# Second layer of a two-layer graph attention: dividing by the row sums per 16 groups instead of per group, and projecting from transposed rows

## The chip, the cores and the metric

The kernel runs on one core of one Trainium2 chip, in float32 throughout. The metric is the time of one execution on the device in microseconds (us).

## The reference, cut to what matters

Two layers of attention over a graph of 4096 nodes with 512 features, 8 heads of 64 each. Only the second is touched here:

```python
h = relu(layernorm(x))                        # x: output of layer 0
keys, queries, values = per head h @ Wk, h @ Wq, h @ Wv
atts = queries @ keys.T / 8 - 1e16 * (1 - max(adj, eye))   # (8, 4096, 4096)
atts = softmax(atts, axis=-1)
x = x + einsum('hqm,hmk,hko->qo', atts, values, Wo)
```

The softmax is exp(score - extreme of the row) divided by the sum of the row. The division can be done at any time before the projection with Wo, since it is one factor per row and head.

## The kernel before, in words

The first layer, the layer norm and the projections to queries, keys and values end at about 2600 us; queries and keys lie transposed in DRAM (`qk_d`), values in `v_d`, the first layer's output in `x1_d`.

The second layer's attention works on `HC` = 4 pairs of heads c (2 x 64 = 128 rows of the transposed output), and in each on `NG` = 32 groups g of 128 query rows. A group has `GS` = 4 steps of 32 queries; so there are `total` = 512 steps. In a step the 128 partitions hold 32 queries times four quarters of the 4096 keys, and the free axis holds 1024 keys for each of the two heads. Stages of several groups overlap: in the loop over s, step s makes the scores of step s (`scores`, TensorE, L856; `masked`, VectorE, adds the penalty from PSUM into the ring `t`, L872), the exponentials of step s-3 (`exps`, ScalarE, L907, whose accumulator output is the sum of each partition), the transposes of step s-4 (`squares` on VectorE by 32x32 blocks, L914; `turned` on TensorE, L920, with the copy `taken` on ScalarE, L926), and a quarter of the product with the values for the group of step s-8 (`weighted`, L937, into one PSUM tile `o`). In every odd step the partial minima of two steps are combined over the four quarters (`parted` on POOL, L881, then `smallest`, L891 and L896). In head pair 0 the penalty is made from adj (`with_self` L838, `made_penalty` L842 and L843) and kept in DRAM (`pen_d`); the later pairs load it.

`finish` closes a group in the two steps after its last product: ScalarE copies `o` (128 rows of two heads by 128 queries) to SBUF as `oT` (L947), four small products on TensorE with `band` add the sums of the four quarters (`den`, L950), VectorE inverts them (L954), TensorE transposes `oT` (`back`, L957), VectorE multiplies (L959), and a DMA stores 128 rows by 128 columns in `att_d` (L963).

The order of instructions on every engine is the order written in the loop (`manual_schedule`); an engine that waits holds all that is written behind it. All loads and stores go through SP's queue, in order too; penalties are requested `AHEAD` = 5 steps before use, into 6 buffers `a`.

When all groups are done, a second stage projects: for each of 32 row blocks it loads `at` (L1050) and `xt` (L1048), transposes four squares of `at` on TensorE (L1053), copies them on ScalarE (L1055), multiplies by `wot` (L1058), adds on VectorE (L1061) and stores (L1062). `wot` is loaded at its start through ScalarE's queue (L1045).

Of the kernel before, what the change touches and what calls it, by code (L numbers as in the profile page):

```python
# [8 lines left out]
F32 = mybir.dt.float32  # L9
# [3 lines left out]
PSUM = bass.MemoryType.PSUM  # L13
DRAM = bass.MemoryType.DRAM

P = 128
# [7 lines left out]
def kernel(  # L24
# [14 lines left out]
    nc = tc.nc  # L39
    N, DM = x.shape  # L40
    H, D = src_proj.shape[1:]
    HD = H * D
    NB = N // P
    KC = DM // P
    HC = HD // P
# [6 lines left out]
    dram = ctx.enter_context(tc.tile_pool(name="dram", bufs=1, space=DRAM))  # L52

    ident = const.tile([P, P], F32, name="ident")
# [5 lines left out]
    SQ = 32  # L60
    NS = P // SQ
    band = const.tile([P, SQ], F32, name="band")
    nc.vector.tensor_reduce(band, ident.rearrange("p (a j) -> p j a", j=SQ), AX.X, ALU.add)
    bands = const.tile([P, P], F32, name="bands")
# [9 lines left out]
    x1_d = dram.tile([N, DM], F32, name="x1_d")  # L74
# [16 lines left out]
    PR = 2 * D  # L91
# [5 lines left out]
    with tc.tile_pool(name="a0k", bufs=1) as pk, tc.tile_pool(name="a0v", bufs=4) as pv, tc.tile_pool(  # L97
        name="a0a", bufs=3
    ) as pa, tc.tile_pool(name="a0t", bufs=7) as pt, tc.tile_pool(name="a0p", bufs=4) as pp, tc.tile_pool(
        name="a0x", bufs=1  # L100
    ) as px, tc.tile_pool(name="a0s", bufs=4) as psb, tc.tile_pool(
        name="a0tr", bufs=3, space=PSUM
# [103 lines left out]
        def finish(G):  # L206

            rows, cols = bass.ts(G.g, P), bass.ts(G.c, PR)
            xt = px.tile([P, PR], F32, name="xt")
            nc.sync.dma_start(xt, x[rows, cols])  # L210
            oT = px.tile([P, P], F32, name="oT")
            nc.vector.tensor_copy(oT, G.o[:, :P])
            den = psb.tile([P, 2], F32, name="den")
            nc.vector.reciprocal(den, G.sm)
            yield
            back = G.o[:, P:]
            nc.tensor.transpose(back, oT, ident)
            yield
            att = px.tile([P, 2, D], F32, name="att")
            nc.vector.tensor_mul(  # L220
                att, back.rearrange("p (h d) -> p h d", d=D), den.unsqueeze(2).to_broadcast([P, 2, D])
            )
            nc.gpsimd.tensor_add(xt, xt, att.rearrange("p h d -> p (h d)"))
            nc.sync.dma_start(x1_d[rows, cols], xt)
# [162 lines left out]
        groups = [Group(c, g) for c in range(PAIRS) for g in range(NB)]  # L387
        total = len(groups) * 2
# [4 lines left out]
        with tc.manual_schedule():  # L393
            NQ = NB // XR
            TB = 8
            rows = [load_rows(0)]
            wn, col = load_wn()
            rows.append(load_rows(1))
            for q in range(NQ + 4):
# [10 lines left out]
                n = q - 3  # L410
# [14 lines left out]
            for s in range(total + 6):  # L425
                G, h = step(s) if s < total else (None, 0)
                for half in range(2):
# [8 lines left out]
                    q = 2 * s + half  # L436
# [320 lines left out]
            while jobs:  # L757
                work()
    l0.close()
    att_d = dram.tile([N, HD], F32, name="att_d")  # L760
    pen_d = dram.tile([N // 32, P, N // 4], F32, name="pen_d")

# [5 lines left out]
    VC = 768  # L770
    NV = VC // SQ
    NT = (QK_ - VC) // P
    with tc.tile_pool(name="a1t", bufs=1) as pt, tc.tile_pool(name="a1k", bufs=4) as pkk, tc.tile_pool(
        name="a1v", bufs=GS
    ) as pv, tc.tile_pool(name="a1a", bufs=6) as pa, tc.tile_pool(name="a1q", bufs=2) as pq, tc.tile_pool(
        name="a1x", bufs=1
    ) as px, tc.tile_pool(name="a1s", bufs=6) as psb, tc.tile_pool(
        name="a1sc", bufs=4, space=PSUM
    ) as psc, tc.tile_pool(name="a1tr", bufs=1, space=PSUM) as ptr, tc.tile_pool(
        name="a1m", bufs=2, space=PSUM  # L780
    ) as pm, tc.tile_pool(name="a1o", bufs=1, space=PSUM) as po:
        t = pt.tile([P, RING, 2, QK_], F32, name="t")
        class Group:


# [115 lines left out]

        def exps(G, k):
            if k == 0:
                G.sm = psb.tile([P, GS, 2], F32, name="sm")
            for h in range(2):
                u = t[:, G.ring + k, h, :]
                nc.scalar.activation(  # L907
                    u, u, AF.Exp, bias=G.nm[k // 2][:, k % 2, h : h + 1], scale=-1.0,
                    accum_out=G.sm[:, k, h : h + 1],
                )  # L910

        def squares(G, k):
# [29 lines left out]
                    )  # L942

        def finish(G):

            oT = px.tile([P, P], F32, name="oT")
            nc.scalar.copy(oT, G.o[:, :P])  # L947
            den = pm.tile([P, 512], F32, tag="ms", name="den")
            for k in range(GS):
                nc.tensor.matmul(  # L950
                    den[bass.ts(k, SQ), :2], lhsT=band, rhs=G.sm[:, k, :], start=True, stop=True
                )
            rden = psb.tile([P, 2], F32, name="rden")
            nc.vector.reciprocal(rden, den[:, :2])  # L954
            yield
            back = pm.tile([P, 512], F32, tag="ms", name="back")
            nc.tensor.transpose(back[:, :P], oT, ident)  # L957
            att = px.tile([P, 2, D], F32, name="att")
            nc.vector.tensor_mul(  # L959
                att, back[:, :P].rearrange("p (h d) -> p h d", d=D),  # L960
                rden.unsqueeze(2).to_broadcast([P, 2, D]),
            )
            nc.sync.dma_start(  # L963
                att_d[bass.ts(G.g, P), bass.ts(G.c, PR)], att.rearrange("p h d -> p (h d)")
            )

        groups = [Group(c, g) for c in range(HC) for g in range(NG)]
        total = len(groups) * GS
# [12 lines left out]
        with tc.manual_schedule():  # L981
            pens = {}

            def prefetch(n):
                if n < total:
                    if n % (QG * GS) == 0:
                        load_queries(n // (QG * GS))
                    pens[n] = penalty(*step(n))

            AHEAD = 5  # L990
            ending = iter(())
            load_keys(0)
            for n in range(AHEAD):
                prefetch(n)
            with_self(*step(0), pens[0])
            made_penalty(*step(0), pens[0])
            for i in range(GS):
                load_values(0, i)
            for s in range(total + PROD + 3):
                if s + 1 < total:  # L1000
                    with_self(*step(s + 1), pens[s + 1])
                if s < total:
                    keep_penalty(*step(s), pens[s])

                c, at = divmod(s + 4, SETS)
                if 0 < c < HC and at == 0:
                    load_keys(c)
                c, at = divmod(s - PROD - 1 + GS, SETS)
                if 0 < c < HC and at < GS:
                    load_values(c, at)  # L1010
                turn = 0 <= s - TURN < total
                if turn:
                    squares(*step(s - TURN))
                    tr = turned(*step(s - TURN))

                if s % 2 and 0 <= s - 3 < total:
                    G, k = step(s - 3)
                    smallest(G, k // 2)
                next(ending, None)
                if s < total:  # L1020
                    scs = scores(*step(s))
                    masked(*step(s), scs, pens.pop(s))
                if turn:
                    taken(*step(s - TURN), tr)
                if 0 <= s - EXPS < total:
                    exps(*step(s - EXPS))
                if s + 1 < total:
                    made_penalty(*step(s + 1), pens[s + 1])
                if s % 2 and s < total:
                    G, k = step(s)  # L1030
                    parted(G, k // 2)
                n = s - PROD
                if 0 <= n < total:
                    W, w = step(n)
                    weighted(W, w)
                    if w == GS - 1:
                        ending = finish(W)
                prefetch(s + AHEAD)


    with tc.tile_pool(name="p3c", bufs=1) as pc, tc.tile_pool(name="p3", bufs=4) as pw, tc.tile_pool(
        name="p3t", bufs=3, space=PSUM
    ) as pst, tc.tile_pool(name="p3m", bufs=3, space=PSUM) as psm:
        wot = pc.tile([P, HC, DM], F32, name="wot")
        nc.scalar.dma_start(wot, wo.rearrange("h d o -> (h d) o").rearrange("(c p) o -> p c o", p=P))  # L1045
        for rb in range(NB):
            xt = pw.tile([P, DM], F32, name="xt")
            nc.sync.dma_start(xt, x1_d[bass.ts(rb, P), :])  # L1048
            at = pw.tile([P, HD], F32, name="at")
            nc.sync.dma_start(at, att_d[bass.ts(rb, P), :])  # L1050
            tr = pst.tile([P, 512], F32, name="atr")
            for c in range(HC):
                nc.tensor.transpose(tr[:, bass.ts(c, P)], at[:, bass.ts(c, P)], ident)  # L1053
            aT = pw.tile([P, HD], F32, name="aT")
            nc.scalar.copy(aT, tr)  # L1055
            o = psm.tile([P, 512], F32, name="oo")
            for c in range(HC):
                nc.tensor.matmul(  # L1058
                    o, lhsT=aT[:, bass.ts(c, P)], rhs=wot[:, c, :], start=(c == 0), stop=(c == HC - 1)
                )  # L1060
            nc.vector.tensor_add(xt, xt, o)  # L1061
            nc.sync.dma_start(out[bass.ts(rb, P), :], xt)  # L1062


# [26 lines left out]
```

## Time and profile before

| | us |
|---|---|
| median of 3 runs (lowest to highest) | 5093.84 (5091.9 to 5098.46) |
| the profiled execution, its own time | 5095.06 |
| its span, first to last instruction | 5093.2 |
| TensorE matmul busy | 4812.7 (94% of the span) |
| VectorE busy | 4541.1 (89%) |
| ScalarE busy | 3928.1 (77%) |
| POOL (GpSimd) busy | 376.7 (7%) |

The mean granted clock of TensorE is 0.982 of full speed. Busy shares are means over a first layer, a second one and a projection with different limits, so they don't say what an edit in one of these is worth. In the lists, PE is TensorE's multiplying, PEld its weight loads beside it, DVE is VectorE, ACT is ScalarE, SP the queue that issues DMAs. A float32 product shows as two records. In lists of groups of instructions, the name before the arrow is the tile written, the names after it are read; "idle before" is the time in which the engine stood still just before.

### The profile page before, as it was taken

To read this page: it belongs to the slowest core of one execution; us is meant where nothing else is said; L and a number is where in the kernel's file an instruction comes from. 1 tells how busy PE (TensorE), PEld (TensorE's weight loads), DVE (VectorE), ACT (ScalarE), POOL (GpSimd) and SP (SyncE) were. 2 spreads that over 40 slices of the span, in tenths; PEclk is the share of its full clock that TensorE was granted. 3 is DMA by queue.
4 is the path that set the end of the run, shared out by engine and by line. 5 is a ranking of instruction groups with operands and counts; after the bars stand their busy time and mean duration, and the time that the engine had idled before them with its cause. 6 is when DMAs were issued, how large, how long until landed. Compare 5 with 4: busy or idle time off the path is not lost.

```text
span 5093.2 us, 145280 instructions
## 1 busy us (share of the span) xinstructions
PE 4812.7 (94%) x61850; PEld 3471.2 (68%) x61850; DVE 4541.1 (89%) x8125; ACT 3928.1 (77%) x4581; POOL 376.7 (7%) x632
## 2 busy tenths in 40 slices
PE   7999999999999959999989999999999999999999
PEld 3588888888888847677756666666666666666664
DVE  4599999999999989888759999999999999999971
ACT  3499999999999988888748888666666666666651
POOL 2000000000000011111112222000000000000000
PEclk9999999999999979999999999999999999999999
DMA  4344353344443364444367777544343343533325
GB/s 157 129 142 140 127 190 132 134 142 169 147 142 128 126 161 136 138 142 138 107 205 239 240 239 239 167 128 127 126 159 126 125 126 128 157 125 126 127 94 178
DMA packets 316152, 764.83 MB, mean 150 GB/s; under 512 B 54448, under 2 KB 156848, under 8 KB 290416
## 3 DMA queue, kind: packets, MB, share of 16 engines
q1 hardware_dynamic: 314976, 754.49, 46.1%
q8 instruction: 486, 7.96, 0.7%
q14 instruction: 162, 1.33, 0.1%
q10 hardware_dynamic: 528, 1.05, 0.1%
HBM read 629.41 MB, written 125.96 MB: 148 GB/s over the span
## 4 chain that ended last, share of the span: by engine, by line
PE 55%; DVE 20%; ACT 14%; issue 7%; DMA 4%; SPq 1%; POOL 0%; DVEq 0%; ACTq 0%; POOLq 0%
PE o L937 18%; PE sc L856 18%; DVE t L154 6%; DVE pT L188 6%; PE tr L920 6%; ACT t L143 4%; ACT t L164 3%; DVE bt L557 3%; PE oo L1058 2%; ACT pT L186 2%; PE mp L357 2%; PE tr L177 2%; DVE bt L596 2%; PE o L199 2%; ACT bt L589 1%
## 5 line engine op out<-in xcount | busy, mean ns | idle before, releaser
L872 DVE CUSTOM_DVE_ANT_0 t<-sc,a 128x512 f32<-128x512 f32 x2048 | 1291.4, 686 | 77.3 <-issue 55.3
L907 ACT ACTIVATE t<-t,nm 128x1024 f32<-128x1024 f32 x1024 | 1168.5, 1143 | 163.7 <-DVE nm L896 163.7
L937 PEld LDWEIGHTS o<-t,v 128*64 128x64 f32 x16384 | 883.9, 137 | 423.7 <-issue 337.7
L856 PE MATMUL sc<-k,q 64*32 64x512 f32 x16384 | 1003.1, 597 | 9.4 <-DVE nm L872 9.4
L937 PE MATMUL o<-t,v 128*64 128x128 f32 x16384 | 1007.1, 276 | 0.2 <-ACT oT L947 0.2
L914 DVE STREAM_TRANSPOSE t<-t 128x1536 f32<-128x1536 f32 x512 | 908.2, 1774 | 8.9 <-ACT t L907 5.9
L154 DVE CUSTOM_DVE_ANT_0 t<-t,a 128x2048 f32<-128x2048 f32 x384 | 876.5, 2282 | 18.0 <-DMA a<-in_adj_dram 18.0
L177 PE MATMUL tr<-ident,t 128*128 128x128 f32 x6144 | 782.6, 277 | 103.3 <-ACT pT L186 91.9
L164 ACT ACTIVATE t<-t,nm 128x4096 f32<-128x4096 f32 x192 | 786.7, 4097 | 27.5 <-DVE nm L159 27.5
L143 ACT ACTIVATE t<-tb,src 128x4096 f32<-128x4096 f32 x192 | 786.2, 4096 | 19.0 <-PE mp L357 17.4
L177 PEld LDWEIGHTS tr<-ident,t 128*128 128x128 f32 x6144 | 664.0, 141 | 198.8 <-ACT pT L186 115.1
L199 PE MATMUL o<-pT,v 128*64 128x128 f32 x12288 | 757.1, 276 | 0.3 <-DVE pT L188 0.3
L199 PEld LDWEIGHTS o<-pT,v 128*64 128x64 f32 x12288 | 664.4, 137 | 64.0 <-issue 63.0
L188 DVE COPY pT<-tr 128x1024 f32<-128x1024 f32 x549 | 657.4, 1217 | 40.4 <-PE tr L177 33.5
L926 ACT COPY t<-tr 128x512 f32<-128x512 f32 x512 | 299.1, 584 | 483.4 <-PE tr L920 478.6
L856 PEld LDWEIGHTS sc<-k,q 64*32 64x32 f32 x16384 | 251.2, 106 | 342.0 <-issue 299.6
L920 PE MATMUL tr<-ident,t 128*128 128x128 f32 x2048 | 342.7, 287 | 10.9 <-ACT t L907 9.2
L547 ACT ACTIVATE lk<-tb,srcb 128x1024 f32<-128x1024 f32 x256 | 281.9, 1112 | 80.8 <-DVE nm L557 73.9
L186 ACT COPY pT<-tr 128x1024 f32<-128x1024 f32 x219 | 302.6, 1382 | 52.1 <-DMA d_d<-d 36.1
L596 DVE STREAM_TRANSPOSE bt<-bt 128x2048 f32<-128x2048 f32 x128 | 295.1, 2306 | 30.0 <-ACT bt L589 30.0
L557 DVE CUSTOM_DVE_ANT_0 bt<-lk,ba 128x1024 f32<-128x1024 f32 x256 | 302.1, 1215 | 22.0 <-ACT e L681 11.2
L589 ACT ACTIVATE bt<-bt,nm 128x1024 f32<-128x1024 f32 x256 | 290.3, 1135 | 0.4 <-DVE nm L578 0.3
(113 smaller groups left out, 3911.2 us busy)
## 6 DMA issues: line engine op xcount, KB each, us to landing
a<-in_adj_dram SPq DMA_DIRECT2D x192, 1024.0 KB, 5.6
a<-pen_d SPq DMA_DIRECT2D x384, 512.0 KB, 3.8
ba<-in_adj_dram SPq DMA_DIRECT2D x512, 128.0 KB, 2.9
a<-in_adj_dram SPq DMA_DIRECT2D x512, 128.0 KB, 3.3
pen_d<-a SPq DMA_DIRECT2D x128, 512.0 KB, 3.4
qk_d<-e SPq DMA_DIRECT2D x64, 256.0 KB, 2.2
x<-in_x_dram SPq DMA_DIRECT2D x8, 1024.0 KB, 5.7
d_d<-d SPq DMA_DIRECT2D x16, 512.0 KB, 2.9
```

The costliest lines, as they stand in the source:

```text
L143: nc.scalar.activation(t, targets[G.c, h], AF.Prelu, bias=src[:, G.g, 2 * G.c + h : 2 * G.c + h + 1], alpha=SLOPE)
L154: nc.vector.tensor_tensor_reduce(out=t, in0=t, in1=rows_of_adj[G, f], scale=-1.0, scalar=FMAX, op0=ALU.add, op1=ALU.min, accum_out=nm[:, f ...
L164: nc.scalar.activation(G.t[h], G.t[h], AF.Exp, bias=G.nm[h][:, NCH : NCH + 1], scale=-1.0, accum_out=G.sm[:, h : h + 1],)
L177: nc.tensor.transpose(tr[:, bass.ts(b % 4 * 2 + h, P)], G.t[h][:, bass.ts(i * MB + b, P)], ident)
L188: nc.vector.tensor_copy(pT, tr)
L199: nc.tensor.matmul(G.o[h * D : (h + 1) * D, :P], lhsT=feats[G.c][i][:, b, bass.ts(h, D)], rhs=pT[:, bass.ts(b % 4 * 2 + h, P)], start=(mb ...
L856: nc.tensor.matmul(sc[h][bass.ts(a, SQ), :], lhsT=G.q[bass.ts(h, D), bass.ds(G.q0 + k * SQ, SQ)], rhs=keys[G.c][half][bass.ts(h, D), a, :] ...
L872: nc.vector.tensor_tensor_reduce(out=t[:, G.ring + k, h, cols], in0=scs[half][h], in1=a[:, cols], scale=1.0, scalar=FMAX, op0=ALU.add, op1 ...
L907: nc.scalar.activation(u, u, AF.Exp, bias=G.nm[k // 2][:, k % 2, h : h + 1], scale=-1.0, accum_out=G.sm[:, k, h : h + 1],)
L914: nc.vector.transpose(u, u)
L920: nc.tensor.transpose(tr[:, bass.ts(h * NT + m, P)], t[:, G.ring + k, h, bass.ds(VC + m * P, P)], ident)
L937: nc.tensor.matmul(G.o[bass.ts(h, D), :P], lhsT=v[:, b, bass.ts(h, D)], rhs=t[:, bass.ds(G.ring, GS), h, bass.ds(at, SQ)], start=(mb == 0) ...
```

## The change

`finish` is now only the copy of `o` and a store of it, still transposed and undivided: `att_d` becomes [4, 128, 4096]. The sums of all head pairs are kept in one tile `sums`, by halves of 16 groups. One step after the last group of a half is finished, a generator `divided` begins and advances once a step: `inverted` adds the quarters of all 16 groups in one product, inverts them on VectorE, transposes them and stores one row of reciprocals per head (`inv_d`); `scaled` then loads four pieces of 512 columns of `att_d` with the reciprocals broadcast over the 64 rows of each head, multiplies them on POOL (on VectorE for the last half) and stores them back.

The projection takes the stored columns as its stationary operand with no transposes. It is written into the loop: from the second step without scores on, each step has one row block, in PSUM tiles of the scores; the rest follows the loop. Loads are by chunks of two blocks, three chunks ahead; the chunks of the second half of the rows are requested only after the last half of the last head pair is scaled. `wot` is loaded in the middle of the last head pair, in a buffer of the keys.

```diff
@@ -757,8 +757,12 @@
             while jobs:
                 work()
     l0.close()
-    att_d = dram.tile([N, HD], F32, name="att_d")
+    att_d = dram.tile([HC, P, N], F32, name="att_d")
+    inv_d = dram.tile([HC, 2, N], F32, name="inv_d")
     pen_d = dram.tile([N // 32, P, N // 4], F32, name="pen_d")
@@ -770,16 +774,19 @@
     VC = 768
     NV = VC // SQ
     NT = (QK_ - VC) // P
+    SG = NG // 2
     with tc.tile_pool(name="a1t", bufs=1) as pt, tc.tile_pool(name="a1k", bufs=4) as pkk, tc.tile_pool(
         name="a1v", bufs=GS
     ) as pv, tc.tile_pool(name="a1a", bufs=6) as pa, tc.tile_pool(name="a1q", bufs=2) as pq, tc.tile_pool(
-        name="a1x", bufs=1
-    ) as px, tc.tile_pool(name="a1s", bufs=6) as psb, tc.tile_pool(
+        name="a1x", bufs=2
+    ) as px, tc.tile_pool(name="a1s", bufs=6) as psb, tc.tile_pool(name="a1z", bufs=2) as pz, tc.tile_pool(name="a1at", bufs=3) as pat, tc.tile_pool(
         name="a1sc", bufs=4, space=PSUM
     ) as psc, tc.tile_pool(name="a1tr", bufs=1, space=PSUM) as ptr, tc.tile_pool(
         name="a1m", bufs=2, space=PSUM
     ) as pm, tc.tile_pool(name="a1o", bufs=1, space=PSUM) as po:
         t = pt.tile([P, RING, 2, QK_], F32, name="t")
+        sums = pt.tile([P, HC, 2, 2, SG, GS], F32, name="sums")
         class Group:
@@ -901,12 +908,12 @@
         def exps(G, k):
             if k == 0:
-                G.sm = psb.tile([P, GS, 2], F32, name="sm")
+                G.sm = sums[:, G.c, G.g // SG, :, G.g % SG, :]
             for h in range(2):
                 u = t[:, G.ring + k, h, :]
                 nc.scalar.activation(
                     u, u, AF.Exp, bias=G.nm[k // 2][:, k % 2, h : h + 1], scale=-1.0,
-                    accum_out=G.sm[:, k, h : h + 1],
+                    accum_out=G.sm[:, h, k : k + 1],
                 )
         def squares(G, k):
@@ -942,27 +949,88 @@
                     )
         def finish(G):
             oT = px.tile([P, P], F32, name="oT")
             nc.scalar.copy(oT, G.o[:, :P])
-            den = pm.tile([P, 512], F32, tag="ms", name="den")
-            for k in range(GS):
+            nc.sync.dma_start(att_d[G.c, :, bass.ts(G.g, P)], oT)
+        def inverted(c, half):
+            tot = pm.tile([P, 512], F32, tag="ms", name="tot")
+            nc.tensor.matmul(
+                tot[:, : 2 * SG * GS], lhsT=bands,
+                rhs=sums[:, c, half].rearrange("p h g k -> p (h g k)"), start=True, stop=True,
+            )
+            inv = px.tile([P, P], F32, tag="oT", name="inv")
+            nc.vector.reciprocal(inv[:SQ], tot[:SQ, : 2 * SG * GS])
+            yield
+            invT = pm.tile([P, 512], F32, tag="ms", name="invT")
+            nc.tensor.transpose(invT[:, :SQ], inv[:SQ], ident[:SQ, :SQ])
+            rows = px.tile([P, SQ], F32, name="rows")
+            nc.scalar.copy(rows, invT[:, :SQ])
+            for h in range(2):
+                nc.sync.dma_start(
+                    inv_d[c, h, bass.ts(half, SG * P)].rearrange("(q i) -> q i", i=SQ), rows[bass.ts(h, D)]
+                )
+            yield
+        def scaled(c, half):
+            last = (c, half) == (HC - 1, 1)
+            zs = []
+            for i in range(4):
+                cols = bass.ts(half * 4 + i, 4 * P)
+                z = pz.tile([P, 2, 4 * P], F32, tag="z", name="z")
+                nc.sync.dma_start(z[:, 0], att_d[c, :, cols])
+                for h in range(2):
+                    nc.sync.dma_start(z[bass.ts(h, D), 1], inv_d[c, h, cols].partition_broadcast(D))
+                yield
+                zs.append((cols, z))
+                if i % 2 == 0:
+                    continue
+                yield
+                for cols, z in zs:
+                    (nc.vector if last else nc.gpsimd).tensor_mul(z[:, 0], z[:, 0], z[:, 1])
+                yield
+                for cols, z in zs:
+                    nc.sync.dma_start(att_d[c, :, cols], z[:, 0])
+                zs = []
+        def divided(c, half):
+            yield from inverted(c, half)
+            yield from scaled(c, half)
+        ZR = 2
+        chunks = []
+        def load_chunk():
+            i = len(chunks)
+            if i >= NG // 2 // ZR:
+                for d in divisions:
+                    for _ in d:
+                        pass
+                divisions.clear()
+            if i < NB // ZR:
+                at = pat.tile([P, HC, ZR * P], F32, name="at")
+                nc.sync.dma_start(at, att_d[:, :, bass.ts(i, ZR * P)].rearrange("c p n -> p c n"))
+                xt = pa.tile([P, ZR, DM], F32, tag="a", name="xt")
+                nc.sync.dma_start(xt, x1_d[bass.ts(i, ZR * P), :].rearrange("(r p) d -> p r d", p=P))
+                chunks.append((at, xt))
+        def projected(j):
+            if j >= NB:
+                return
+            i, r = divmod(j, ZR)
+            at, xt = chunks[i]
+            o = psc.tile([P, HF], F32, tag="sc", name="oo")
+            for c in range(HC):
                 nc.tensor.matmul(
-                    den[bass.ts(k, SQ), :2], lhsT=band, rhs=G.sm[:, k, :], start=True, stop=True
-                )
-            rden = psb.tile([P, 2], F32, name="rden")
-            nc.vector.reciprocal(rden, den[:, :2])
-            yield
-            back = pm.tile([P, 512], F32, tag="ms", name="back")
-            nc.tensor.transpose(back[:, :P], oT, ident)
-            att = px.tile([P, 2, D], F32, name="att")
-            nc.vector.tensor_mul(
-                att, back[:, :P].rearrange("p (h d) -> p h d", d=D),
-                rden.unsqueeze(2).to_broadcast([P, 2, D]),
-            )
-            nc.sync.dma_start(
-                att_d[bass.ts(G.g, P), bass.ts(G.c, PR)], att.rearrange("p h d -> p (h d)")
-            )
+                    o, lhsT=at[:, c, bass.ts(r, P)], rhs=wot[:, c, :], start=(c == 0), stop=(c == HC - 1)
+                )
+            nc.vector.tensor_add(xt[:, r], xt[:, r], o)
+            if r == ZR - 1:
+                nc.sync.dma_start(out[bass.ts(i, ZR * P), :].rearrange("(r p) d -> p r d", p=P), xt)
+                load_chunk()
         groups = [Group(c, g) for c in range(HC) for g in range(NG)]
         total = len(groups) * GS
@@ -988,7 +1056,8 @@
                     pens[n] = penalty(*step(n))
             AHEAD = 5
-            ending = iter(())
+            rb = 0
+            divisions = []
             load_keys(0)
             for n in range(AHEAD):
                 prefetch(n)
@@ -1016,7 +1085,12 @@
                 if s % 2 and 0 <= s - 3 < total:
                     G, k = step(s - 3)
                     smallest(G, k // 2)
-                next(ending, None)
+                n = s - PROD
+                if 0 < n <= total and n % GS == 0:
+                    finish(groups[n // GS - 1])
+                if s > total:
+                    projected(rb)
+                    rb += 1
                 if s < total:
                     scs = scores(*step(s))
                     masked(*step(s), scs, pens.pop(s))
@@ -1029,37 +1103,23 @@
                 if s % 2 and s < total:
                     G, k = step(s)
                     parted(G, k // 2)
-                n = s - PROD
                 if 0 <= n < total:
                     W, w = step(n)
                     weighted(W, w)
-                    if w == GS - 1:
-                        ending = finish(W)
+                if n > 1 and n % (SG * GS) == 1:
+                    divisions.append(divided(*divmod(n // (SG * GS) - 1, 2)))
+                for d in divisions[:1]:
+                    if next(d, d) is d:
+                        divisions.pop(0)
+                if s == (HC - 1) * SETS + SETS // 2:
+                    wot = pkk.tile([P, HC, DM], F32, tag="k", name="wot")
+                    nc.sync.dma_start(wot, wo.rearrange("h d o -> (h d) o").rearrange("(c p) o -> p c o", p=P))
+                if s > total - AHEAD and len(chunks) < 3:
+                    load_chunk()
                 prefetch(s + AHEAD)
-    with tc.tile_pool(name="p3c", bufs=1) as pc, tc.tile_pool(name="p3", bufs=4) as pw, tc.tile_pool(
-        name="p3t", bufs=3, space=PSUM
-    ) as pst, tc.tile_pool(name="p3m", bufs=3, space=PSUM) as psm:
-        wot = pc.tile([P, HC, DM], F32, name="wot")
-        nc.scalar.dma_start(wot, wo.rearrange("h d o -> (h d) o").rearrange("(c p) o -> p c o", p=P))
-        for rb in range(NB):
-            xt = pw.tile([P, DM], F32, name="xt")
-            nc.sync.dma_start(xt, x1_d[bass.ts(rb, P), :])
-            at = pw.tile([P, HD], F32, name="at")
-            nc.sync.dma_start(at, att_d[bass.ts(rb, P), :])
-            tr = pst.tile([P, 512], F32, name="atr")
-            for c in range(HC):
-                nc.tensor.transpose(tr[:, bass.ts(c, P)], at[:, bass.ts(c, P)], ident)
-            aT = pw.tile([P, HD], F32, name="aT")
-            nc.scalar.copy(aT, tr)
-            o = psm.tile([P, 512], F32, name="oo")
-            for c in range(HC):
-                nc.tensor.matmul(
-                    o, lhsT=aT[:, bass.ts(c, P)], rhs=wot[:, c, :], start=(c == 0), stop=(c == HC - 1)
-                )
-            nc.vector.tensor_add(xt, xt, o)
-            nc.sync.dma_start(out[bass.ts(rb, P), :], xt)
+            for j in range(rb, NB):
+                projected(j)
 # ---- launch: one core; inputs and outputs as the reference has them ----
```

## The prediction, made before the change was run

> **What bounds the kernel now.** I read the busy shares by stage first, then the chain of waits in a piece of the second layer, then the order of time on TensorE and VectorE there, and last the chain over the end. By stage (window, length, then busy us of PE, PEld, DVE, ACT, POOL; clock, DMA share, GB/s):
>
> ```profile
> 2620.00:4926.80 2306.80, 2292.74 (x36037) 1426.67 (x36021) 2218.09 (x5200) 1617.18 (x2788) 188.91 (x378) 1.00 0.50 160
> 4926.80:4957.40 30.60, 20.66 (x308) 17.31 (x306) 8.22 (x11) 10.63 (x20) 0.24 (x1) 0.92 0.27 95
> 4957.40:5093.20 135.80, 130.43 (x380) 62.75 (x380) 22.02 (x32) 16.69 (x31) 0.00 (x0) 0.98 0.54 174
> ```
>
> The second layer's attention fills 2307 us with PE busy 99% and DVE 96%; then 31 us of draining, and 136 us of projection, in which DVE and ACT are nearly idle. Busy PE alone proves little, so I took the chain of waits from 3400 to 3500 us:
>
> ```profile
> by line: PE o L937 42.8%; PE sc L856 41.3%; PE tr L920 12.9%; PE nmB L891 1.6%; PE den L950 0.9%; PE back L957 0.7%
> ```
>
> Only PE stands on it: one PE instruction after another. So whatever PE no longer does is gained there, if the next engine allows it. PE in order of time, one group (start, length):
>
> ```profile
> 3203.78 1.95 PE L856 MATMUL sc<-k,q 64*32 64x512 f32 x32
> ...
> 3208.28 1.95 PE L856 MATMUL sc<-k,q 64*32 64x512 f32 x32
> ...
> 3212.64 0.24 PE L950 MATMUL den<-sm,band 128*32 128x2 f32 x8
> 3212.82 1.95 PE L856 MATMUL sc<-k,q 64*32 64x512 f32 x32
> ...
> 3217.23 0.31 PE L957 MATMUL back<-ident,oT 128*128 128x128 f32 x1
> 3217.47 1.95 PE L856 MATMUL sc<-k,q 64*32 64x512 f32 x32
> ...
> 3221.83 1.95 PE L856 MATMUL sc<-k,q 64*32 64x512 f32 x32
> ```
>
> Distances of the sc starts: 4.50 (a step with the minimum, nmB), 4.54 (with den), 4.65 (nmB and back), 4.36 (plain). They repeat through head pairs 1 to 3. So den costs 4.54 - 4.36 = 0.18 us of PE per group, back 4.65 - 4.50 = 0.15 us. The end, as the chain:
>
> ```profile
> 4948.96 6.50 DMA at<-att_d
> 4957.36 6.22 PE oo L1058 x8
> 4964.69 7.13 PE oo L1058 x16
> 4972.72 2.41 PE oo L1058 x5
> ```
>
> The projection starts with a wait for its load; then two blocks (16 records) take 8.03 us from start to start, of which 7.13 are product and the rest the transposes atr. A block's product alone is 8 x 0.43 = 3.43 us.
>
> **What the Trainium skill says.** "SBUF — State Buffer", section "Who interferes with whom": a VectorE instruction with at most one SBUF input and outside the two-port modes doesn't contend with GpSimd; one with two SBUF inputs does. The trace agrees: POOL's sum L223, 458 ns as a rule, took up to 2407 ns in the first layer, where the masking L154 reads two SBUF tiles; the second layer's masking L872 reads PSUM and one SBUF tile, and its mean is 684 ns in head pair 0, beside POOL's 1.05 us L843 in each step, and 687 ns later. "GPSIMD Engine Reference", "3.1 Elementwise — side-by-side cycle accounting": a two-input operation on 2048 elements takes 4497 ns, 2.2 ns an element; the trace gives (458 - 239) / 96 = 2.3 between L223 (128) and L881 (32). "TensorE: Matmul & The Clock Gate", "What's actually happening": an idle window of about 3.4 us drops the clock to half. The trace agrees: after 6.3 us of idle the first oo block took 6.22 instead of 3.43 us.
>
> **The change part by part.** All against the profiled execution: span 5093.2, its time 5095.06, 1.2 above the median 5093.84.
>
> *Removed per group:* den and back on PE, 0.33 us. Head pairs 1 to 3: 96 x 0.33 = 31.7 us. On DVE the reciprocal L954 (0.13) and product L959 (0.28) go too. Would DVE take over as bound? Four steps of it without them are 2 x (2.45 masking + 1.70 squares + 0.26 for the minimum) + 2 x (2.45 + 1.81) = 17.3 us against PE's 4.36 + 4.50 + 4.36 + 4.50 = 17.7. No, by 2%. In head pair 0 DVE also adds the diagonal (L838, 0.18) and a group takes 18.05 early and 18.35 late (3010.5 to 3028.8), where transposes wait 0.3 us for exps that a late DVE delays. There the gain is 0.33 x 32 = 10.6 if only PE's work goes, 20 if the wait goes as well; DVE's own 0.41 less some gaps gives about 12, which I take. Together 44 us.
>
> *The output copy* L947 stays on ACT, at the same place of the step. Its store now follows ACT's copy instead of DVE's product, one step earlier; on SP only loads for five steps ahead (22 us) queue behind it. Nothing.
>
> *inverted*, seven times in the steps (the eighth is in the tail): a sum of two records and 128 columns, about 0.3 us on PE (nmB with 32 columns costs 0.14, a transposed 128 columns 0.15 a record), a small transpose, 0.15; DVE waits some 0.3 us for the sum, queued with its next squares behind it, and ACT copies 64 columns in the idle that ends at its tr. 7 x 0.75 = 5 us lost at most; I take 5. Net of the steps: 39 us.
>
> *scaled* for seven halves: 28 products on POOL at 0.24 + 480 x 0.0023 = 1.3 us, 37 us in all, next to an engine with 7% of work; only the parts L881 and, in head pair 0, the penalty L843 queue behind them, and a pair of products (2.7 us) sits in a step without parts. By the SBUF rule and the PSUM operand of L872 no DVE cost; if the squares did block, at most 37 us (upper end). SP issues 28 x 4 more DMAs at 0.32 to 0.65 us, and stops for a store (about 2.2 us) before each second pair, against 22 us of lead: nothing. A gain from them is excluded, since they add work.
>
> *The weights* load at half of the last head pair instead of behind it: hidden, DMA share 0.4 there.
>
> *The drain and the projection.* Before, from the transposes of the first step without scores (4929.46) to the end: 163.7 us. After, PE by steps: first 1.65 to the end of its waits, + 3.43 + 1.90 = 7.0; two steps with tr, oo, o at 0.59 + 3.43 + 1.90 = 5.92; four with oo and o at 5.33; three with oo alone, and the last sum: 10.7. That is 50.8 us for ten blocks; 22 more at 3.43 are 75.5: 126.3. The transposes and the copy aT are gone, the ACT waits of the drain are filled.
>
> Then what is late next: the last half. Its scaling is issued when block 11's sum is stored, and the load of chunk 8 (block 16) stands behind it on SP. From there: six issues 2.8, landing 3.6 (row at<-att_d), products 0.7 each on DVE, store 2.2, the second pair once more since there are two z buffers (issues, landing, product, store issue about 8), load 3.8 (row a<-pen_d, same size): about 20 us. PE has blocks 12 to 15 meanwhile, 13.7. The gap, about 7, brings the half clock once more, 2.8. Bounds 0 to 20; taken 10. Last sum and a store of 512 KB: 4.3, before 3.6. Sum 126.3 + 10 + 4.3 = 140.6: 23 us gained.
>
> Total 39 + 23 = 62: 5093.84 - 62 = 5032 us.
>
> **Rivals.** *The tail gives nothing* (5055): a chunk is 1 MB in and 0.5 MB out per 6.86 us, 229 GB/s, where the projection ran at 174 GB/s with DMA busy 54%: scaled, 71%, and att_d now comes in pieces of 1 KB instead of 2. If a chunk takes 8.5 us, 11 of them eat 18 us. Against: head pair 0 moves 240 GB/s at 74%, and 4950 to 4960 us shows 342.
> *Slower:* the same mechanism decided by size. PE waits on each chunk when its 1.5 MB need more than 6.86 us; from 6.86 + 62 / 11 = 12.5 us (126 GB/s) the whole gain is gone, and at 14 us the time is about 5111. Against it: no window with loads outstanding runs that low.
> *Only the tail gains* (5071): another engine sets the steps as soon as PE gets shorter, which DVE's 96% speaks for, the 17.3 against 17.7 and the PE-only chain against.
> *More than forecast* (5018): the whole wait of head pair 0 goes and the tail's gap is closed by early loads.
> *It doesn't do what it says:* the products can't hang behind anything but DMA; if tiles are tracked coarsely, each sum would wait for the exps of its step, below 2 us seven times, inside the range.
>
> **How the numbers follow.** Forecast 5032: 0.64. Tail nothing: 0.15, 5055. More: 0.09, 5018. Only the tail: 0.06, 5071. Slower: 0.06. A measurement of this kernel can tell about 0.2%, 10 us. From the cases: faster 0.91, within 0.2% 0.03, slower 0.06. The range takes in the bounds of head pair 0, of the gap and of the chunks: 5012 to 5064.
>
> **What would show it.** Right: steps of 4.36 and 4.50 alternating in all four positions of a group; no DVE wait behind POOL; a single gap of 5 to 10 us of PE between blocks 15 and 16; blocks 3.43 us apart after it. Wrong: sc starts still 18.05 per group (another bound); L914 or L872 longer while POOL multiplies; PE waiting on at for every second block (DMA); penalty loads arriving late around a half's scaling (SP's queue).

## The result, and the profile after

| | before | after |
|---|---|---|
| median of 4 runs (lowest to highest), us | 5094.59 (5091.9 to 5098.46) | 5050.41 (5047.76 to 5051.5) |
| profiled span, us | 5093.2 | 5047.6 |
| ratio, with 95% interval | | 0.9912 (0.9895 to 0.9929) |

The change gains 44 us, 0.9%; 62 were forecast. Busy time by stage of the changed kernel (columns as in the table of before: window, length, busy us of PE, PEld, DVE, ACT, POOL, then clock, DMA share, GB/s):

```profile
2620.00:4903.00 2283.00, 2265.43 (x34977) 1403.79 (x34977) 2195.33 (x4957) 1619.53 (x2800) 223.60 (x407) 1.00 0.55 173
4903.00:4955.00 52.00, 51.31 (x325) 28.33 (x321) 12.27 (x14) 8.17 (x17) 0.00 (x0) 1.00 0.38 124
4955.00:4976.00 21.00, 20.94 (x49) 9.06 (x49) 3.45 (x5) 0.18 (x1) 0.00 (x0) 1.00 0.64 204
4976.00:4985.70 9.70, 0.03 (x1) 0.06 (x1) 3.77 (x6) 0.00 (x0) 0.00 (x0) 0.72 0.71 185
4985.70:5047.00 61.30, 57.51 (x128) 25.11 (x128) 10.98 (x16) 0.00 (x0) 0.00 (x0) 0.96 0.60 209
```

The drain is full now (PE 51.31 of 52 us), and there is one hole, in the fourth row. In the chain of waits from 3400 to 3500 us, den and back are gone from a list that is still PE's alone:

```profile
by line: PE o L944 43.1%; PE sc L863 42.6%; PE tr L927 12.9%; PE nmB L898 1.6%
```

and the starts of the scores (PE in order of time, late in head pair 3) lie 4.51 and 4.36 us apart by turns, in all four positions of a group:

```profile
4883.49 1.95 PE L863 MATMUL sc<-k,q 64*32 64x512 f32 x32
...
4888.00 1.95 PE L863 MATMUL sc<-k,q 64*32 64x512 f32 x32
...
4892.36 1.95 PE L863 MATMUL sc<-k,q 64*32 64x512 f32 x32
...
4896.87 1.95 PE L863 MATMUL sc<-k,q 64*32 64x512 f32 x32
```

To see where the gain arises, take the starts of the squares on VectorE (L914, now L921), one for each step, 16 steps apart, as us per group:

| steps | before | after |
|---|---|---|
| 16 to 31 | 18.19 | 18.05 |
| 32 to 63 | 18.34 | 18.30 |
| 64 to 79, in which half 0 is divided | 18.35 | 18.73 |
| 80 to 111 | 18.35 | 18.32 |
| 112 to 127 | 18.05 | 17.95 |
| head pairs 1 to 3, sixteen steps with a division | 18.05 | 17.90 |
| head pairs 1 to 3, all others | 18.05 | 17.73 |

Head pairs 1 to 3 give what was forecast. Head pair 0 gives nothing: from the squares of step 16 to the first of head pair 1 both kernels take 511.9 us. From the first step without scores to the end the time falls from 163.7 us (4929.46 to 5093.2) to 144.4 (4903.17 to 5047.6).

### The profile page after: what moved, and what is told of

Read it like the earlier page. It is cut to its first block, busy times and chain, and to the rows that moved or that the text cites. A ratio compares the mean times of both kernels' runs of the same rounds, so it can differ in the third digit from the quotient of the medians.

```text
span 5047.6 us, 142850 instructions
## 1 busy us (share of the span) xinstructions
PE 4762.2 (94%) x60594; PEld 3428.8 (68%) x60594; DVE 4518.4 (90%) x7881; ACT 3910.9 (77%) x4557; POOL 411.2 (8%) x660
## 4 chain that ended last, share of the span: by engine, by line
PE 52%; DVE 19%; ACT 15%; issue 8%; DMA 4%; SPq 1%; POOL 1%; DVEq 0%; ACTq 0%; POOLq 0%
PE sc L863 17%; PE o L944 17%; DVE t L154 6%; DVE pT L188 6%; PE tr L927 5%; ACT t L143 4%; ACT t L164 3%; DVE bt L557 3%; PE tr L177 2%; ACT pT L186 2%; PE mp L357 2%; DMA a<-in_adj_dram 2%; PE o L199 2%; PE oo L1027 2%; ACT bt L589 2%
## 5 line engine op out<-in xcount | busy, mean ns | idle before, releaser
L914 ACT ACTIVATE t<-t,nm 128x1024 f32<-128x1024 f32 x1024 | 1168.0, 1143 | 179.8 <-DVE nm L903 179.8
L921 DVE STREAM_TRANSPOSE t<-t 128x1536 f32<-128x1536 f32 x512 | 907.7, 1773 | 5.0 <-ACT t L914 2.0
L164 ACT ACTIVATE t<-t,nm 128x4096 f32<-128x4096 f32 x192 | 797.0, 4151 | 27.5 <-DVE nm L159 27.5
L143 ACT ACTIVATE t<-tb,src 128x4096 f32<-128x4096 f32 x192 | 796.4, 4149 | 19.2 <-PE mp L357 17.4
L177 PEld LDWEIGHTS tr<-ident,t 128*128 128x128 f32 x6144 | 664.2, 141 | 198.9 <-ACT pT L186 113.6
L186 ACT COPY pT<-tr 128x1024 f32<-128x1024 f32 x219 | 313.9, 1433 | 52.1 <-DMA d_d<-d 36.2
L927 PEld LDWEIGHTS tr<-ident,t 128*128 128x128 f32 x2048 | 213.5, 140 | 116.6 <-issue 84.1
```

The costliest lines, as they stand in the source:

```text
L143: nc.scalar.activation(t, targets[G.c, h], AF.Prelu, bias=src[:, G.g, 2 * G.c + h : 2 * G.c + h + 1], alpha=SLOPE)
L164: nc.scalar.activation(G.t[h], G.t[h], AF.Exp, bias=G.nm[h][:, NCH : NCH + 1], scale=-1.0, accum_out=G.sm[:, h : h + 1],)
L177: nc.tensor.transpose(tr[:, bass.ts(b % 4 * 2 + h, P)], G.t[h][:, bass.ts(i * MB + b, P)], ident)
L914: nc.scalar.activation(u, u, AF.Exp, bias=G.nm[k // 2][:, k % 2, h : h + 1], scale=-1.0, accum_out=G.sm[:, h, k : k + 1],)
L921: nc.vector.transpose(u, u)
L927: nc.tensor.transpose(tr[:, bass.ts(h * NT + m, P)], t[:, G.ring + k, h, bass.ds(VC + m * P, P)], ident)
```

## The circle in head pair 0

These lines are engines mixed, in order of time, from head pair 0 of the changed kernel; each waits for what stands above it, but for the squares of 2808.57, which are shown for the distance to the masking (the second exponential and the rest of the masking are left out):

```profile
2805.72 0.15 DVE L903 TENSOR_REDUCE nm<-nmB 128x4 f32<-128x32 f32 x1
...
2805.91 1.15 ACT L914 ACTIVATE t<-t,nm 128x1024 f32<-128x1024 f32 x1 [1.25 <-DVE nm L903]
...
2808.19 1.04 ACT L849 ACTIVATE a<-a 128x1024 f32<-128x1024 f32 x1
...
2808.57 1.78 DVE L921 STREAM_TRANSPOSE t<-t 128x1536 f32<-128x1536 f32 x1
...
2809.31 1.04 POOL L850 TENSOR_SCALAR a<-a 128x1024 f32<-128x1024 f32 x1 [4.40 <-DMA a<-in_adj_dram]
...
2810.39 0.69 DVE L879 CUSTOM_DVE_ANT_0 t<-sc,a 128x512 f32<-128x512 f32 x1
...
2812.96 0.18 DVE L845 TENSOR_TENSOR a<-a,ident 32x32 f32<-32x32 f32 x1
...
2813.17 1.78 DVE L921 STREAM_TRANSPOSE t<-t 128x1536 f32<-128x1536 f32 x1
...
2814.87 0.15 DVE L903 TENSOR_REDUCE nm<-nmB 128x4 f32<-128x32 f32 x1
```

The minimum releases two exponentials on ACT; the relu of the next penalty stands behind them on ACT; POOL makes the penalty of it (2809.31 to 2810.35); the masking waits for that; the diagonal and the squares stand behind the masking on VectorE; and the next minimum behind them. 2814.87 - 2805.72 = 9.15 us for two steps, 18.30 a group. (The profile puts POOL's wait down to a DMA of adj here, and in most other steps to the relu, which ended 0.08 us before POOL began.) VectorE waits very little in this circle: the masking starts 1.82 us after the squares of 2808.57, and where it waits for nothing it follows in 1.70.

No work of den, rden or back lies on this circle. In the kernel before, head pair 0 takes 9.15 and 9.19 us for two steps by turns. In the 9.15 the masking starts 0.04 us after POOL is done (2810.19 + 1.04), and the small reciprocal of den only fills the wait for it:

```profile
2809.44 1.78 DVE L914 STREAM_TRANSPOSE t<-t 128x1536 f32<-128x1536 f32 x1
...
2810.19 1.04 POOL L843 TENSOR_SCALAR a<-a 128x1024 f32<-128x1024 f32 x1 [4.41 <-DMA q<-qk_d]
...
2811.14 0.13 DVE L954 RECIPROCAL rden<-den 128x2 f32<-128x2 f32 x1
2811.27 0.69 DVE L872 CUSTOM_DVE_ANT_0 t<-sc,a 128x512 f32<-128x512 f32 x1
```

In the 9.19, which hold the product att (L959), VectorE has no such wait: they are as long as its own work. So two limits of head pair 0 lay side by side in the kernel before: the circle, 18.30 us a group, and VectorE's own work with den and back, by estimate 18.31 (the 17.98 that e2 below shows without them, 0.13 for the reciprocal, 0.20 for the product). PE's own 18.05 was just below both. The change lowers VectorE's work and PE's, and leaves the circle. That is the theory; the rivals for the 18.30 of the changed kernel were VectorE's own work and the DMA of adj.

## The experiments

All are edits of the changed kernel unless they say otherwise; their ratios are against the kernel before.

**e1, the diagonal on POOL.** In `with_self`:

```diff
-                nc.vector.tensor_max(diag, diag, ident[...])
+                nc.gpsimd.tensor_add(diag, diag, ident[...])
```

> The changed kernel with the diagonal of adj (L845, head pair 0 only) handled by POOL instead of VectorE; POOL adds the identity where VectorE takes the maximum, so the diagonal's values differ. Theory A (a circle of waits holds head pair 0: exps and relu on ACT, penalty on POOL, masking, diagonal and squares on VectorE, minimum, exps again, 9.15 us per two steps): the circle loses about 0.33 us per two steps and falls below PE's 8.86, so late groups of head pair 0 fall from 18.30 to 17.7-17.8 us and the time to about 5037. Theory B (the DMA of adj or ACT's own work holds head pair 0): groups stay at 18.3, time 5050. Theory C (POOL's order gets worse because the diagonal queues behind the penalty): groups above 18.3, time over 5055.

Where adj already has a 1 on its diagonal, and its random zeros and ones have it in about half of the rows, the sum is 2 and the penalty comes out as -1e16 instead of 0. So e1, e6 and e8, which all add, measure where the time goes; they don't compute the reference. e9, with the tail of e8, does.

5031.23 us, ratio 0.9876 (0.986 to 0.9893). Squares in steps 16 to 63 lie at 17.73 us a group, 0.57 less than the 18.30 of steps 32 to 63 in the changed kernel, and the chain of waits from 2800 to 2900 us is PE's alone:

```profile
by line: PE sc L863 42.7%; PE o L944 42.5%; PE tr L927 13.5%; PE nmB L898 1.6%
```

DMA and ACT kept all their work, so theory B falls, although the profile's own chain for 2780 to 2880 us of the changed kernel had put 23.1% on the DMA of adj. The edit also takes work from VectorE, so it can't tell the circle from VectorE's own work; e2 does. The gain of 19 us is some 6 more than these groups and the later ones explain; the rest lies at the start, where the first squares came 11.5 us earlier (2617.4 instead of 2628.9) and the first sixteen steps took 6 us longer. Part of that can be chance: in the runs that change nothing up to there (the changed kernel, e3, e4, e5, e7) the squares of step 16 start anywhere from 2696.7 to 2700.3 us, with the diagonal on POOL at 2694.2, and at 2693.2 in e8.

**e2, the relu ahead of the exponentials.** Two blocks of the loop change places:

```diff
-                if 0 <= s - EXPS < total: exps(...)
                 if s + 1 < total: made_penalty(...)
+                if 0 <= s - EXPS < total: exps(...)
```

> The changed kernel with the relu of the next penalty (L849) written ahead of the exponentials on ACT, so that POOL's penalty no longer waits for them. Theory A (circle through exps, relu, POOL, masking): the circle is cut there; VectorE's own work, 9.0 us per two steps with the diagonal, is next, so 18.30 goes to about 18.05 and the time to 5044; but if the even step's exponentials, now 1.04 us later, make PE wait for its transposes, groups may come out longer than 18.3 and the time up to 5060. Theory B (VectorE's own work, with no wait, holds head pair 0): 18.30 stays, 5050.

5042.64 us, ratio 0.9899 (0.9884 to 0.9913). Groups of 17.98 in steps 32 to 63 and 18.00 in 80 to 111: the circle is cut, no work is taken away, and VectorE stands without a wait. The masking follows the squares in 1.70 us:

```profile
2802.42 1.78 DVE L921 STREAM_TRANSPOSE t<-t 128x1536 f32<-128x1536 f32 x1
2804.12 0.15 DVE L903 TENSOR_REDUCE nm<-nmB 128x4 f32<-128x32 f32 x1
2804.20 0.67 DVE L879 CUSTOM_DVE_ANT_0 t<-sc,a 128x512 f32<-128x512 f32 x1
...
2806.96 1.78 DVE L921 STREAM_TRANSPOSE t<-t 128x1536 f32<-128x1536 f32 x1
2808.66 0.65 DVE L879 CUSTOM_DVE_ANT_0 t<-sc,a 128x512 f32<-128x512 f32 x1
```

Theory B, VectorE's own work behind 18.30, falls: the same work fits in 18.0. PE shows as busy throughout here too, but e1 has the same PE work in 17.73; so what holds these groups at 18.0 is most likely VectorE's own work, which no further run tested.

**e6, the diagonal on POOL in the kernel before** (the edit of e1).

> The kernel before, with only the diagonal of adj moved to POOL (POOL adds where VectorE takes the maximum, so the diagonal's values differ). Theory A (the circle and PE's own work stood within 2% of each other in head pair 0; the change shortened PE and left the circle): groups of head pair 0 go from 18.35 only to PE's own 18.05, about 24 x 0.3 = 7 us, with the start up to 5 us more: 5082 to 5088. The change is then worth about 50 us or more once the diagonal is on POOL in both. Theory B (the diagonal on POOL gains the same in either kernel): 19 us, 5075.

5083.42 us, ratio 0.9979 (0.9972 to 0.9987). Groups from 18.35 to PE's own 18.05, as theory A said. The edit shortens VectorE's work and the circle alike, so it doesn't tell which of the two held the kernel before. Without both the change is worth 5083.4 - 5031.2 = 52 us, 8 more than it gained with the circle; in the profiles about 4 us of this difference lie before step 16, where runs vary.

**e4, all of the scaling on VectorE.**

```diff
-                    (nc.vector if last else nc.gpsimd).tensor_mul(z[:, 0], z[:, 0], z[:, 1])
+                    nc.vector.tensor_mul(z[:, 0], z[:, 0], z[:, 1])
```

> The changed kernel with all 32 products of the scaling on VectorE instead of 28 of them on POOL: 28 x 0.69 us more VectorE work. Theory A (POOL's products cost nothing since VectorE's masking reads PSUM; VectorE has 2% to spare): a pair of 1.4 us in one step outlasts what PE has in hand, 0.5 to 1.4 us per pair are lost: 5057 to 5069. Theory B (POOL's products do hold VectorE up now, so moving them costs no more): 5050 or less.

5060.55 us, ratio 0.9934 (0.992 to 0.9949): 10 us slower than with POOL. Per half of head pairs 1 to 3, the sixteen steps with a division grow by 4 x (18.36 - 17.90) = 1.8 us, of which the next sixteen win 0.3 back; in head pair 0 they grow by 4 x (20.03 - 18.73) = 5.2. That is 14 us for seven halves; 3 of them are hidden by chance, as this run reached step 16, where nothing is edited, 3.1 us earlier.

**e7, no division.** `divided` is never appended to `divisions`.

> The changed kernel with the division left out: no inverted, no scaled, so rows stay undivided. It measures what the division still costs. Theory A (0.67 us per half in head pairs 1 to 3, 1.8 in head pair 0, and the gap with its half clock in the tail, about 12.5 us): about 18 us less, 5032, groups of head pairs 1 to 3 at 17.73 throughout, no gap ahead of block 16. Theory B (the gap is supply of chunks, not the division): only 6 us less, 5044.

5029.59 us, ratio 0.9874 (0.9857 to 0.989): the division costs 21 us in all, 18 were expected. All groups of head pairs 1 to 3 lie at 17.73, so its part there is 4 x 0.17 = 0.67 us a half. There is no gap ahead of block 16: the chunks alone keep PE busy, and the gap is the division's.

**e3, the last half pair by pair.** In `load_chunk`, where the changed kernel runs `scaled` to its end before chunk 8:

```diff
-            if i >= NG // 2 // ZR:
-                for d in divisions: ...run to its end...
+            if i >= NG // 2 // ZR and divisions:
+                for _ in range(5 if i == NG // 2 // ZR else 1):
+                    next(divisions[0], None)
```

> The changed kernel, where the last half is scaled pair by pair: chunk 8 is requested after the first two pieces are stored, the other two pieces are scaled between the chunks that follow. Theory A (the gap of 9.7 us ahead of block 16 is the SP order: four pieces ahead of one load): chunk 8 is requested about 6.5 us sooner, the gap shrinks to about 3 us, with the half clock mostly gone too; 5041. Theory B (the gap is the time of the loads themselves): gap stays near 9 us, 5050, or the second pair now holds chunk 12 up in a second gap.

5044.49 us, ratio 0.9902 (0.9887 to 0.9917). First the chain over the gap in the changed kernel, then that of e3:

```profile
4966.58 4.41 DMA z<-inv_d
...
4971.83 2.02 DMA att_d<-z
...
4974.99 3.98 DMA z<-inv_d
...
4980.29 5.24 DMA at<-att_d
4985.53 0.14 issue
4985.67 57.56 PE oo L1027 x128
```

```profile
4965.15 4.74 DMA z<-inv_d
...
4970.73 2.04 DMA att_d<-z
...
4974.35 5.54 DMA at<-att_d
4979.90 0.14 issue
4980.03 56.88 PE oo L1025 x128
```

One round of loading and scaling is gone from the chain, and the gap shrinks from 9.7 to 3.8 us. No second gap appeared. The half clock was expected to go for the most part, and didn't: the first block after the gap takes 5.20 us, against 5.88 in the changed kernel and 3.43 for the blocks that follow. So the time is 5044.5 and not 5041.

**e5, the projection behind the loop.** The lines `if s > total: projected(rb); rb += 1` are taken out.

> The changed kernel with every row block projected behind the loop, none in its last ten steps. Theory A (what the projection gained is the transposes and the wait for its first load, not the place in the drain): the drain takes about 19 us again as in the kernel before, 32 blocks at 3.43 us are 110, the gap ahead of block 16 stays: about 147 us from the first step without scores instead of 144, so 5053. Theory B (ten blocks were hidden in the drain): ten times 3.43 come back: 5085.

5052.64 us, ratio 0.9919 (0.9904 to 0.9934): 2 us slower than the change, no more than the spread of either kernel's runs. The chain shows the tail without overlap:

```profile
4914.59 7.21 PE o L944 x128
...
4923.55 41.41 PE oo L1027 x96
...
4988.41 57.98 PE oo L1027 x128
```

PE's drain ends at 4922 and the projection starts within 2 us of it, without the 9 us of before, since its chunks are loaded. Theory B falls: the drain without blocks takes 20.5 us (4903.0 to 4923.5), ten blocks behind it 34.4, and the drain with ten blocks in it took 51.9. A block put in there lengthens the drained steps by most of its own time.

**e8, less time than either.** The edits of e1 and e3, with the first two pieces of the last half loaded right behind the loop (so three rounds are left ahead of chunk 8 instead of five):

```diff
+            for _ in range(2):
+                next(divisions[0], None)
             for j in range(rb, NB):
                 projected(j)
```

> A version meant to beat both: diagonal on POOL (adding instead of the maximum), the last half scaled pair by pair, and its first two pieces loaded right behind the loop, ahead of blocks 10 and 11. From 5031 with the diagonal alone: 6 us for the pairs, and if chunk 8 is then requested another 4 us sooner the remaining gap of 3.8 us closes: 5021 to 5025. If the gap stays because the loads land no sooner: 5026 or more.

5020.78 us, ratio 0.9856 (0.9842 to 0.9871): 73 us less than before. In the chain chunk 8 lands at 4957.7, and PE waits 0.9 us for it:

```profile
4943.93 3.00 DMA z<-inv_d
...
4947.77 3.11 DMA att_d<-z
...
4952.45 5.27 DMA at<-att_d
4957.72 0.14 issue
4957.86 55.19 PE oo L1025 x128
```

**e9, the same tail with the edit of e2 instead of e1.**

> The reference's computation in full: the changed kernel with the relu ahead of the exponentials and with the tail of the last best version (last half pair by pair, its first two pieces loaded right behind the loop). If the two gains add: 5042.6 less 10 us of tail, 5032 to 5034. If the tail's gain depends on the diagonal's place: above 5037.

5034.21 us, ratio 0.9884 (0.9868 to 0.9901). The two gains add, to about 2 us: behind the last squares this run takes 122.8 us where e2 takes 132.9, and PE's gap is 1.4 us. The sum of the medians would be 5032.2; its squares of step 16 came 3.7 us later than in e2, ahead of anything that the tail's edit touches.

## Why the prediction was right, and where it was off

The profiled executions differ by 45.6 us where 62 were forecast. Head pair 0, with what lies ahead of it, makes up some 11 of the 16 that are missing, the drain and the projection 4.

- **den and back, head pairs 1 to 3** (31.7 us): 18.05 to 17.73, 96 x 0.32 = 30.7. The reading of distances on PE, and the sum by which VectorE wouldn't take over (17.3 against 17.7), held there.
- **Head pair 0** (12 us): the step that failed. The prediction took the 0.3 us of waiting there as VectorE being late, and from it a gain between PE's 10.6 and 20. VectorE was late, but a circle through three engines that the removed work isn't part of took 18.30 us a group by itself, 0.04 less than what was measured before; so the lower bound should have been near zero. Measured from the first squares to the first of head pair 1: 1.8 us, all of it in the first sixteen steps. From there on nothing is gained: the first division costs the 1.7 us that the other steps save. Another 1.6 us were lost ahead of the first squares, where the change edits nothing.
- **inverted** (5 us for seven): 6 x 0.67 + 1.7 = 5.7. That the sum came so near is partly luck, since a term of it was missing: the reciprocal takes 0.95 us on VectorE, and with the wait for the sum it makes one step 6.05 us instead of 4.50:

```profile
3237.64 0.69 DVE L879 CUSTOM_DVE_ANT_0 t<-sc,a 128x512 f32<-128x512 f32 x1
...
3238.93 0.95 DVE L964 RECIPROCAL inv<-tot 32x128 f32<-32x128 f32 x1 [0.59 <-PE tot L959]
3239.80 1.71 DVE L921 STREAM_TRANSPOSE t<-t 128x1536 f32<-128x1536 f32 x1
```

  The next steps on VectorE (4.06, 4.28, 4.12) make up for most of it.
- **scaled on POOL** (nothing): right. A product took 1.29 us, and in the first pair after 3257 us the squares beside it kept their 1.77. This agrees with what the Trainium skill, "SBUF — State Buffer", section "Who interferes with whom", says of a VectorE instruction with one SBUF input, and e4 shows what the place is worth: 10 us.
- **Drain and projection** (140.6 us): 144.4. The first ten blocks took 51.9 us (50.8 forecast), the other 22 with the gap and the half clock 88.1 (85.5), the end 4.4 (4.3). The gap was 9.7 instead of 7: a loading of reciprocals took 4.0 to 4.4 us, 3.6 were taken, and chunk 8 took 5.2, 3.8 were taken. That the gap would be there, and why, was right. e5 adds what the forecast did not ask: all but some 3 of the 19 us gained in the tail come without the place in the drain, that is, from the transposes and the first wait.
- **Rivals**: what "only the tail gains" said of the whole, that another limit sets the steps once PE is shorter, came true in head pair 0 alone; supply of chunks was never the limit (e7).

## What to carry to other kernels

Ahead of costing removed work at its full length, ask stage by stage whether it lies on what repeats: follow one release from an engine back to itself, and if that circle takes as long as a step, work outside it is worth nothing there. Where limits stand within 2% of each other, as VectorE's work, the circle and PE's work did in head pair 0, lowering some of them is worth the distance to the next that stays, however much work is removed. And where data returns through DRAM, count the rounds (load, compute, store, load) on the one queue: scaling two pieces instead of four before the first dependent load closed 5.9 of 9.7 us, more than the 2.8 that all four products take together.

## What was not expected of the hardware

A reciprocal on VectorE is dear by the column: 0.131 us for 2 columns (L954, before), 0.945 for 128 (L964, after). An estimate from these two sizes is 6.5 ns a column.

The squares that follow the diagonal start 0.11 us after it in the early steps and 0.21 us after it from then on. In order of time, early and late in head pair 0 of the changed kernel:

```profile
2677.53 0.17 DVE L845 TENSOR_TENSOR a<-a,ident 32x32 f32<-32x32 f32 x1
2677.64 1.76 DVE L921 STREAM_TRANSPOSE t<-t 128x1536 f32<-128x1536 f32 x1
```

```profile
2808.36 0.18 DVE L845 TENSOR_TENSOR a<-a,ident 32x32 f32<-32x32 f32 x1
2808.57 1.78 DVE L921 STREAM_TRANSPOSE t<-t 128x1536 f32<-128x1536 f32 x1
```

The change comes with step 32, where the diagonal moves from partitions 0 to 31 to the next 32. The Trainium skill, "VectorE: DVE Perf Modes", section "Two Vector instructions with no wait between them", gives as a model that an instruction whose output or input starts in another group of 32 partitions than the one before is held until that one has finished. The trace fits it: in the early lines the squares start before the diagonal has ended, in the late ones only after. The diagonal itself is later by as much: it began 0.08 us before the end of the masking ahead of it, and from step 32 on begins 0.03 us after it. At the same step the distance of the minima goes from 8.90 to 9.15 us for two steps, and these two delays are 0.22 of it. No run here moved the diagonal within VectorE to test it by itself.

In the step of the first division the reciprocal pushed the diagonal under POOL's penalty, and it took 1.06 us instead of 0.18:

```profile
2945.63 0.95 DVE L964 RECIPROCAL inv<-tot 32x128 f32<-32x128 f32 x1
2946.61 1.06 DVE L845 TENSOR_TENSOR a<-a,ident 32x32 f32<-32x32 f32 x1
2947.70 1.78 DVE L921 STREAM_TRANSPOSE t<-t 128x1536 f32<-128x1536 f32 x1
```

The diagonal reads two SBUF tiles, and POOL's L850 ran from 2946.58 to 2947.62. This agrees with the other half of the rule in "Who interferes with whom": a VectorE instruction with two SBUF inputs does contend with a GpSimd instruction that reads SBUF.
